# Two frequency rows in one PSUM tile, copied by two engines at once into halves of the partitions

## The chip, the cores and the metric

The kernel runs on one core of a Trainium2 chip (trn2). The metric is the device time of one execution in microseconds; the median of three runs is what versions are compared by. A profile records one further execution, with the start and length of each instruction on TensorE (PE, with its weight loads PEld), VectorE (DVE), ScalarE (ACT), GpSimd (POOL) and the queue of SyncE (SP), which issues the loads.

## The reference

The reference is four layers, each added to its input x of 2 images x 128 channels x 64 x 64 pixels, float32: an attention layer, a layer of convolutions, a convolution by Fourier transform and a second attention layer. Only the third, layer 2, is touched. It treats the 128 channels as 32 quaternions of four parts and multiplies in the frequency domain:

```python
xs = jnp.stack([x[:, :q], x[:, q:2 * q], x[:, 2 * q:3 * q], x[:, 3 * q:]])
Xs = jnp.fft.rfft2(xs, s=(GRID_H, GRID_W), axes=(-2, -1))
Ws = jnp.stack([kr_w + 1j * ki_w, kr_x + 1j * ki_x, kr_y + 1j * ki_y, kr_z + 1j * ki_z])
C = jnp.einsum('piohw,qbihw->pqbohw', Ws, Xs)
Pw = C[0, 0] - C[1, 1] - C[2, 2] - C[3, 3]
Px = C[0, 1] + C[1, 0] + C[2, 3] - C[3, 2]
...
o = jnp.fft.irfft2(P, s=(GRID_H, GRID_W), axes=(-2, -1))
```

For each of 64 x 33 frequencies this is a product of a 128 x 32 matrix of weights (real and imaginary) with the spectrum of both images, in four signed arrangements of the parts.

## The kernel before

Layer 2 is `_layer2`, L803. A first part normalizes X and transforms it along the height; the result is `y`, kept in SBUF. A last part transforms back along the height and adds to X. Between them stands the part that the change touches, L897 to L1117. It works on eight blocks `kb` of four frequency rows `m` and their four mirror images, so a block has two halves: first the products of the *direct* rows, then those of the *image* rows. In each half:

- `rows_of_weights` (L819) has SyncE load the weights of four rows, real and imaginary, 2112 KB each, into one of two buffers.
- `products` (L990) runs 17 steps, `j`, one for each pair of frequencies. A step is four matmuls with 32 columns each, one for each of four rows `s`; the trace has two instructions for each, so a step is eight. They multiply the weights by `e`, the copied and signed spectra, into one of four banks `z0` to `z12`, or, for the last step, into a bank of the pool `bank`. After every fourth step VectorE transposes a bank into `z` (L1017), and at the end it combines `z` to `pz` (L1025).
- Beside the products, `alongside` (L1075) takes steps of other generators, so that the next block is prepared and the last one is finished under the products: `rows_in` for two rows of the next block; `turned`, which transposes `pz` (L1037) and copies it to `pzt` (L1044, ScalarE); and in the direct half `back`, which transforms the last block back along the width (L1062) and copies it to `y` (L1065, ScalarE). `alongside` spreads a given number of steps over the 17, and takes what is left over after the last.

`rows_in` (L971) is the preparation. `transposed` (L909) turns a row of `y` by TensorE (L912) and ScalarE copies it to `yt` (L918). `transformed` (L921) multiplies it by a matrix, for both images, into a bank of the tag `pe` (L925), which has two buffers, so each of the two rows has its own. The bank then holds the spectrum of the direct row and of its image row. `copies` and `placed` (L979, L934) write it to `e` for both places. The four quaternion parts lie on four groups of 32 partitions, and each is needed in four arrangements `r` with signs `SIGN2`: part `p` of arrangement `r` comes from part `r ^ p`. That is 12 copies for a row and a place, of 136 elements: one of all 128 partitions with signs from a tile, one of 64 and ten of 32. `together` (L962) alternates two generators: ScalarE makes all copies of the first row (L948), VectorE all of the second (L950), four at a step. So `rows_in` has ten steps for two places, the last of each place without work.

The instructions of an engine run in the order in which the program was written (`_in_order`). Semaphores between the engines are set by the language's tile layer, which also gives out the buffers of a pool in turn: an instruction that needs a buffer waits for the last use of it.

For block 0 all four rows of the direct place are prepared before the first product, and those of the image place beside its direct half; its image half has two `rows_in` beside it, for block 1. Block 7 prepares nothing.

## Time and profile before

| | |
|---|---|
| median of 3 runs | 4103.53 us (4102.0 to 4110.83) |
| the profiled execution | 4101.59 us, of which the span of the profile is 4099.8 us |
| busy over the span | PE 3930.8 us (96%), DVE 3182.8 (78%), ACT 3230.9 (79%), POOL 72.5 (2%) |
| the stretch of the changed code | about 1918 to 2181 us of the span |
| copies to `e`, ScalarE | 384 instructions |
| copies to `e`, VectorE | 384 instructions |

Lines of the profile are read so. The page's second part cuts the span in 40 slices; a digit is the busy share in tenths. The view by stretch gives, for each stretch, its length, then busy microseconds and the count of instructions of PE, PEld, DVE, ACT and POOL, the clock that TensorE was granted, the share of the DMA engines and GB/s. A line of the waits names engine, tile and line that waited, then what ended the wait: microseconds in all, times, the longest. A line of the timeline is start, length, engine, line, instruction, output and input, count, and in brackets the idle time before it with what ended it. A line of the groups gives count, then busy microseconds and mean nanoseconds of one, then the idle time before them. A line of the DMA issues ends with the size in KB and the median time to landing in us.

### The profile page before, as it was taken

Reading aid. Unit: us, or ns where it says so; the run is one execution under the profiler, and the core shown is the slowest. Engines: PE = TensorE matmul, PEld = TensorE weight load, DVE = VectorE, ACT = ScalarE, POOL = GpSimd, SP = SyncE. Lnnn points to the kernel's source line nnn. Section 1 sums busy time; section 2 is a strip of 40 time slices with the busy share of each in tenths; the row PEclk is TensorE's granted clock in tenths of the full one; section 3 lists DMA queues with packets and bytes.
Section 4 is the critical chain, followed back from the end, with each engine's and each line's share of the span. In section 5 each row is a group of like instructions: output and inputs, shape, how many; then the busy total and the mean of one; then the engine's idle time right before and its main releaser. Section 6 shows DMA issues by size and latency. Waiting matters only on the chain. (4 is left out here: it accounts for less than half of the span.)

```text
span 4099.8 us, 83182 instructions
## 1 busy us (share of the span) xinstructions
PE 3930.8 (96%) x35790; PEld 1374.4 (34%) x35790; DVE 3182.8 (78%) x3526; ACT 3230.9 (79%) x3907; POOL 72.5 (2%) x145
## 2 busy tenths in 40 slices
PE   7999999989999998997898999999999999999998
PEld 4522222245222223445565232222222222222222
DVE  4689999856989998986775887777777777776666
ACT  4478888744888884334663899999999999999998
POOL 1001000000000001000000000000000000000000
PEclk9999999999999999998899999999999999999999
DMA  1199980000000000002673211120012101110000
GB/s 50 20 184 178 179 123 2 2 2 2 1 2 2 2 2 13 0 2 100 257 285 116 87 34 32 31 66 27 29 32 63 34 24 32 33 56 6 6 6 4
DMA packets 193133, 217.66 MB, mean 53 GB/s; under 512 B 30441, under 2 KB 154345, under 8 KB 188658
## 3 DMA queue, kind: packets, MB, share of 16 engines
q1 hardware_dynamic: 192754, 212.25, 20.2%
q8 instruction: 282, 4.62, 0.5%
q14 instruction: 97, 0.79, 0.1%
HBM read 178.64 MB, written 98.57 MB: 68 GB/s over the span
## 5 line engine op out<-in xcount | busy, mean ns | idle before, releaser
L2183 ACT ACTIVATE weights<-ps_s 128x1024 f32<-128x1024 f32 x1920 | 1781.7, 1066 | 77.0 <-PE ps_s L2169 76.9
L1381 ACT ACTIVATE weights<-ps_s 128x1024 f32<-128x1024 f32 x1024 | 993.4, 1024 | 170.4 <-PE ps_s L1372 152.3
L2192 PE MATMUL ps_acc<-weights,vt 128*32 128x512 f32 x8192 | 1093.8, 606 | 0.0
L1829 DVE TENSOR_TENSOR sums<-sums,weights 128x2048 f32<-128x2048 f32 x384 | 879.9, 2291 | 45.4 <-ACT weights L1381 9.1
L2169 PE MATMUL ps_s<-q,k 64*128 64x512 f32 x4096 | 831.4, 470 | 4.0 <-DMA k<-stack 2.8
L2169 PEld LDWEIGHTS ps_s<-q,k 64*128 64x128 f32 x4096 | 348.9, 184 | 937.2 <-ACT weights L2183 810.3
L1372 PE MATMUL ps_s<-q,k 32*64 32x512 f32 x8192 | 630.9, 614 | 4.6 <-ACT weights L1381 2.4
L1789 PE MATMUL ps_acc<-weights,vt 128*32 128x512 f32 x4096 | 551.7, 607 | 7.2 <-ACT used L1819 3.7
L2141 DVE SCALAR_TENSOR_TENSOR exp_z<-exp_z,exp_m 128x1024 f32<-128x1024 f32 x384 | 468.9, 1221 | 9.3
L2125 DVE TENSOR_SCALAR exp_i<-ps_s 128x1024 int32<-128x1024 f32 x128 | 156.7, 1224 | 217.2 <-PE ps_s L2169 217.0
L1372 PEld LDWEIGHTS ps_s<-q,k 32*64 32x64 f32 x8192 | 161.8, 130 | 435.6 <-PE ps_s L1372 337.1
L2192 PEld LDWEIGHTS ps_acc<-weights,vt 128*32 128x32 f32 x8192 | 161.9, 108 | 309.8 <-issue 309.4
L1789 PEld LDWEIGHTS ps_acc<-weights,vt 128*32 128x32 f32 x4096 | 81.2, 108 | 427.5 <-issue 404.0
L662 DVE SCALAR_TENSOR_TENSOR X<-g,w,X 128x2048 f32<-128x2048 f32 x84 | 197.3, 2350 | 2.6
L1829 DVE TENSOR_TENSOR sums<-weights 128x2048 f32<-128x2048 f32 x64 | 146.6, 2291 | 63.2 <-ACT weights L1381 62.9
L2145 DVE SCALAR_TENSOR_TENSOR weights<-exp_z,exp_i 128x1024 f32<-128x1024 f32 x128 | 156.8, 1225 | 15.6 <-ACT weights L2183 0.5
L1577 PE MATMUL ps_sp<-pad,diag 32*32 32x512 f32 x4608 | 158.9, 597 | 2.3 <-ACT q L1597 1.3
L2141 DVE SCALAR_TENSOR_TENSOR exp_z<-exp_m 128x1024 f32<-128x1024 f32 x128 | 155.8, 1218 | 0.0
L1008 PE MATMUL ps_z<-w_ri,e 128*32 128x128 f32 x2048 | 137.3, 408 | 14.5 <-DVE e L950 12.3
L1577 PEld LDWEIGHTS ps_sp<-pad,diag 32*32 32x32 f32 x4608 | 96.0, 103 | 53.1 <-issue 15.7
L950 DVE TENSOR_SCALAR e<-ps_pe 32x136 f32<-32x136 f32 (+1 forms) x352 | 104.4, 297 | 5.0
L948 ACT ACTIVATE e<-ps_pe 32x136 f32<-32x136 f32 (+1 forms) x352 | 99.3, 282 | 4.1
(296 smaller groups left out, 2801.4 us busy)
## 6 DMA issues: line engine op xcount, KB each, us to landing
w_ri<-w_r SPq DMA_DIRECT2D x16, 2112.0 KB, 8.1
w_ri<-w_i SPq DMA_DIRECT2D x16, 2112.0 KB, 13.4
stack<-qs SPq DMA_DIRECT2D x64, 256.0 KB, 2.1
q<-stack SPq DMA_DIRECT2D x128, 128.0 KB, 2.5
k<-stack SPq DMA_DIRECT2D x128, 128.0 KB, 2.5
stack<-ks SPq DMA_DIRECT2D x32, 256.0 KB, 2.2
w_r<-in_L_conv_kr_w SPq DMA_DIRECT2D x15, 528.0 KB, 13.7
w_r<-in_L_conv_kr_x SPq DMA_DIRECT2D x15, 528.0 KB, 13.3
```

What stands on the lines that cost most here:

```text
L662: nc.vector.scalar_tensor_tensor(xi, g[:, i : i + H // 2, j : j + W], w8[:, s : s + 1], xi, ALU.mult, ALU.add)
L1372: nc.tensor.matmul(ps[j // 2][to, j % 2, :], k[rows, kt * 128 + 64 * half : kt * 128 + 64 * half + 64], q[rows, qb * CH : (qb + 1) * CH], ...
L1381: nc.scalar.activation(w[:, 2 * p : 2 * p + 2, :], ps[p], AF.Exp)
L1577: nc.tensor.matmul(ps[r // 2][to, r % 2, :].rearrange("p (h w) -> p h w", w=W), diag[rows, grp, t, :], pad[rows, y0 : y0 + ROWS, t % 3 : t ...
L1789: nc.tensor.matmul(ac[n][rows, :], lhs(rows), w[:, j, :], start=first, stop=last)
L1829: nc.vector.tensor_add(parts[0].rearrange("p j c -> p (j c)"), t.rearrange("p j c -> p (j c)"), w.rearrange("p j c -> p (j c)"),)
L2125: nc.vector.tensor_scalar(i, ps.rearrange("p j c -> p (j c)"), EXP_SCALE, EXP_BIAS, ALU.mult, ALU.add)
L2141: nc.vector.scalar_tensor_tensor(z, x, n, m, ALU.add, ALU.mult)
L2145: nc.vector.scalar_tensor_tensor(w.rearrange("p j c -> p (j c)"), z, EXP_TERMS[-1], power, ALU.add, ALU.mult)
L2169: nc.tensor.matmul(ps[j // 2][:, j % 2, :], g.k[kt // 4][rows, j // 2, keys], g.q[qb][rows, j // 2, :], start=True, stop=True,)
L2183: nc.scalar.activation(w[0], ps[p], AF.Exp)
L2192: nc.tensor.matmul(g.ac[32 * j : 32 * j + 32, :], g.vt[:, kt, j // 2, i : i + 2, :].rearrange("p a d -> p (a d)"), w[:, i, :], start=(at = ...
```

## The change

Two rows now share one tile `pe` of two banks, with one buffer in place of two of one bank each. The matmul of an image writes its columns with steps, so that the two images' real and imaginary parts stand side by side, four to a frequency, as they stand in `e`. A copy then takes both rows at once, 272 elements. The work is divided by partitions and no longer by rows: ScalarE writes partitions 0 to 63, VectorE 64 to 127. For two rows and a place ScalarE makes 7 copies and VectorE 6. `e` of the image place keeps the rows in the order in which they come, and `products` reads them from the other end. `together` and `copies` are gone, and `rows_in` has eight steps.

```diff
-        def transformed(m, yt):
-
-            pe = bank("pe")
+        def transformed(m, yt, pe):
+
             for b in range(B):
                 nc.tensor.matmul(
-                    pe[:, b * 8 * PAIRS : (b + 1) * 8 * PAIRS],
+                    pe[:, :, b],
                     yt[:, b, :],
-                    k["fwd_w_both" if m else "fwd_w_ends"],
+                    k["fwd_w_both" if m else "fwd_w_ends"].rearrange("p (x c) -> p x c", c=2),
                     start=True,
                     stop=True,
                 )
-            return pe[:, : B * 8 * PAIRS].rearrange("p (b s f c) -> p b s f c", b=B, s=2, c=2)
-
-        def placed(kb, m, got, image, e, scalar):
-
+
+        def placed(m, got, image, e):
 
 
             row = (m - 1) % 4
-            s, row = (1, 3 - row) if image else (0, row)
 
             def copied(r, p, n=1):
                 to = slice(32 * p, 32 * p + 32 * n)
                 of = slice(32 * (r ^ p), 32 * (r ^ p) + 32 * n)
-                sign = signs if n == 4 else float(SIGN2[r][p])
-                out = e[to, row, :, 4 * r : 4 * r + 4].rearrange("p f (b c) -> p b f c", c=2)
-                sign = sign[to, :] if n == 4 else sign
-                if scalar:
-                    nc.scalar.mul(out, got[of, :, s], sign)
+                sign = signs[to, :] if r == 0 else float(SIGN2[r][p])
+                out = e[to, row : row + 2, :, 4 * r : 4 * r + 4]
+                if p < 2:
+                    nc.scalar.mul(out, got[of, :, image], sign)
                 else:
-                    nc.vector.tensor_scalar_mul(out, got[of, :, s], sign)
-
-            copied(0, 0, 4)
+                    nc.vector.tensor_scalar_mul(out, got[of, :, image], sign)
+
+            copied(0, 0, 2)
+            copied(0, 2, 2)
+            copied(2, 0)
             copied(2, 2, 2)
-            copied(2, 0)
             copied(2, 1)
             yield
             for r in (1, 3):
...
         def rows_in(kb, rows, places, es):
 
             yts = [transposed(m) for m in rows]
             yield
-            gots = [transformed(m, yt) for m, yt in zip(rows, yts)]
+            pe = psp.tile([128, 2, CH], F32, tag="pe", name="ps_pe", bufs=1)
+            pairs = pe[:, :, : B * 8 * PAIRS].rearrange("p m (sf b c) -> p m sf b c", b=B, c=2)
+            got = pe[:, :, : B * 8 * PAIRS].rearrange("p m (s f x) -> p m s f x", s=2, x=2 * B)
+            for n, (m, yt) in enumerate(zip(rows, yts)):
+                transformed(m, yt, pairs[:, n])
             yield
...
             for image in places:
                 if es[image] is None:
                     es[image] = ep.tile([128, 4, 2 * PAIRS, 8 * B], F32, tag="e", name="e")
-                yield from together(
-                    *(
-                        placed(kb, m, got, image, es[image], i % 2 == 0)
-                        for i, (m, got) in enumerate(zip(rows, gots))
-                    )
-                )
-
-        def products(ws, e, pz):
+                yield from placed(rows[0], got, image, es[image])
+
+        def products(ws, e, image, pz):
...
-                        e[:, s, 2 * j : 2 * j + 2, :].rearrange("p f x -> p (f x)"),
+                        e[:, 3 - s if image else s, 2 * j : 2 * j + 2, :].rearrange("p f x -> p (f x)"),
...
-            alongside(products(rows_of_weights(kb, False), e[0], pzs[0]), chain(*side), n)
+            alongside(products(rows_of_weights(kb, False), e[0], 0, pzs[0]), chain(*side), n)
...
-            alongside(products(rows_of_weights(kb, True), e[1], pzs[1]), chain(*side), n)
+            alongside(products(rows_of_weights(kb, True), e[1], 1, pzs[1]), chain(*side), n)
```

More of the change, by code (lines that the diff above doesn't have):

```diff
@@ L960, in placed @@
                 yield
-        def together(*gens):
-            gens = list(gens)
-            while gens:
-                for g in list(gens):
-                    if next(g, gens) is gens:
-                        gens.remove(g)
-                yield
         def rows_in(kb, rows, places, es):
@@ L974, in rows_in @@
             yield
-            gots = [transformed(m, yt) for m, yt in zip(rows, yts)]
+            pe = psp.tile([128, 2, CH], F32, tag="pe", name="ps_pe", bufs=1)
[3 more added lines that the diff above has]
+                transformed(m, yt, pairs[:, n])
             yield
-            yield from copies(kb, rows, gots, places, es)
-        def copies(kb, rows, gots, places, es):
             for image in places:
```

## The prediction

> **What bounds the kernel now.** I read the page's slices first, to see which engine holds each stretch, then the busy time by stretch around the changed code, then its instructions in order of time, then the clock after a wait, then the durations of the copies.

> ```profile
> span 4099.8 us, 83182 instructions
> PE   7999999989999998997898999999999999999998
> w_ri<-w_i SPq DMA_DIRECT2D x16, 2112.0 KB, 13.4
> ```

> TensorE is the busy engine nearly everywhere. The changed code runs from 1918 to 2181 us alone. The last line is half of a weight load: it lands 13.4 us after issue. The same stage by stretch (busy us and instructions of each engine, the granted clock, DMA share, GB/s):

> ```profile
> 1918.30:1970.00 51.70, 34.80 (x358) 22.80 (x358) 35.53 (x107) 32.90 (x110) 0.00 (x0) 0.79 0.30 115
> 1970.00:2153.60 183.60, 173.53 (x2061) 116.16 (x2064) 133.78 (x368) 114.69 (x347) 0.00 (x0) 0.92 0.70 276
> ```

> The first row is the fill (the first two row pairs and block 0), the second six like blocks, 1 to 6, at 183.6/6 = 30.6 us. There TensorE is busy 95%; VectorE (73%) and ScalarE (62%) work beside it. TensorE's waits in the second row:

> ```profile
> PE ps_z L1008 <- DVE e L950: 6.6, 6, 2.1
> PE ps_bank L1062 <- ACT y L1065: 4.8, 6, 0.8
> ```

> So at most 11.4 us can be won there, 0.3%. One block in order of time (TensorE, VectorE, ScalarE):

> ```profile
> 2050.17 0.64 PE L1008 MATMUL ps_z<-w_ri,e 128*32 128x128 f32 x8
> ...
> 2052.04 1.19 PE L925 MATMUL ps_pe<-consts,yt 128*128 128x136 f32 x8
> 2053.27 0.36 DVE L950 TENSOR_SCALAR e<-ps_pe,signs 128x136 f32<-128x136 f32 x1 [4.52 <-PE ps_pe L925]
> 2053.20 3.23 ACT L948 ACTIVATE e<-ps_pe 64x136 f32<-64x136 f32 x11
> 2060.10 0.58 ACT L1044 COPY pzt<-ps_bank 66x512 f32<-66x512 f32 x1
> ```

> The reader is to see that ScalarE and VectorE copy at the same time, each from its own bank, and that ScalarE's pzt copy comes only after its copies. Last, what follows a wait of TensorE (slices: busy us, granted clock, DMA share, GB/s):

> ```profile
> 1945.00:1947.00 2.00, 0.00 (x0) 0.54 0.88 338
> ...
> 1953.00:1955.00 2.00, 2.00 (x44) 1.00 0.97 405
> ```

> ```profile
> 1947.52 0.67 PE L1008 MATMUL ps_z<-w_ri,e 128*32 128x128 f32 x8 [4.38 <-DVE e L950]
> 1949.32 2.18 PE L925 MATMUL ps_pe<-consts,yt 128*128 128x136 f32 x8
> ...
> 1985.91 3.63 PE L1062 MATMUL ps_bank<-consts,pzt 66*128 66x128 f32 x16 [0.81 <-ACT y L1065]
> ```

> A wait of 4.38 us brings the clock to a half until some 5 us after its end. L925 then takes 2.18 us, not 1.19, and L1062 3.63, not 2.05; a product group (8 matmuls) starts every 0.5 us at either clock.

> **The change part by part.** Durations of what it replaces and of the nearest larger reads from PSUM (mean ns behind the comma):

> ```profile
> L950 DVE TENSOR_SCALAR e<-ps_pe 32x136 f32<-32x136 f32 x320 | 95.0, 297 | 4.5
> L948 ACT ACTIVATE e<-ps_pe 32x136 f32<-32x136 f32 x320 | 90.3, 282 | 3.7
> L948 ACT ACTIVATE e<-ps_pe,signs 128x136 f32<-128x136 f32 x32 | 12.1, 379 | 17.9 <-PE ps_pe L925 17.7
> L918 ACT COPY yt<-ps_bank 128x256 f32<-128x256 f32 x36 | 12.9, 374 | 26.8 <-PE ps_bank L912 26.3
> L1065 ACT COPY y<-ps_bank 128x512 f32<-128x512 f32 x14 | 10.1, 723 | 38.0 <-PE ps_bank L1062 38.0
> L876 DVE COPY gt<-ps_pt 128x512 f32<-128x512 f32 x1 | 0.7, 691 | 1.0 <-PE ps_pt L870 1.0
> ```

> *Count and length of copies.* For two rows and one place (direct or image) ScalarE and VectorE each issued 12 copies of 136 elements; now ScalarE issues 7 and VectorE 6 of 272. ScalarE: 374 ns at 256 elements and 587 at 512 (the copies L884 and L1140) give 0.83 ns an element, so 272 cost 0.395 us, with signs 0.49. VectorE: (691-297)/376 = 1.05 ns an element, so 0.44, with signs 0.50 (that copy took 0.36 behind a wait, 0.06 more). As busy time: 2.86 and 2.70 us a group against 3.6 and 3.7. Bounds: no cost for the added elements (0.28 and 0.30); strided as L1065 (0.47).

> *Side by side becomes one behind the other.* Both engines now read the same two-bank tile. In the built program each access to it from one engine waits for the last access from the other: A, D, A, D, AAA, DD, AA, DD (A a ScalarE copy, D a VectorE copy), and the next group's first A for the last D. That is 8 hand-overs a group. Hand-overs between these engines in this trace:

> ```profile
> 13.29 0.16 DVE L1508 SCALAR_TENSOR_TENSOR gn_shift<-gn_got 128x1 f32<-128x1 f32 x1 [0.67 <-POOL gn_got L1403]
> 13.49 0.81 ACT L1515 ACTIVATE g<-X,gn_shift,gn_got 128x512 f32<-128x512 f32 x1 [7.52 <-DVE gn_shift L1508]
> ```

> 13.45 to 13.49 is 0.04 us. Group: 2.86 + 2.70 + 8 x 0.04 + 5 x 0.01 between copies of one engine + 3 x 0.04 (a VectorE copy after a wait took 0.36, in a row 0.32) = c = 6.05 us, where the two together took 3.75. Bounds of c: 4.4 (elements free), 6.95 (strided, hand-overs 0.05 dearer, the length of a semaphore event on TensorE's queue). I take 6.05: its rows read PSUM on the same engines.

> [...] No row here shows two engines in one bank; the built waits are by bank.

> *Image half* (products of the mirrored rows; L1008 to L1008). Start to end of L925 is 3.05 us (2050.17 to 2053.23). Then 0.05, two groups 12.1, and 0.15 for a transpose of 0.72 that stands between the groups in VectorE's queue, of which the next A covers all but that: copies end at 15.35. The next direct half needs them for its rows 2 and 3. Behind ScalarE's last copy (14.35) queues the pzt copy, 0.58, which frees the bank for the last product (0.5 us): TensorE ends at 15.45. TensorE's own work is 11.3 (2050.17 to the end of the last product at 2060.95, and one L1037 of 0.56 that moves in from behind it).

> *Direct half.* VectorE still has two transposes of 0.72 and one of 0.28 after its last copy, which free the bank of the second row: TensorE waits about 0.75, L925 ends at 3.4. Two groups: 15.55; ScalarE's last copy 14.55; pzt 15.2. rows_in now has 8 steps, not 10, so the back-transforms (L1062, 2.05 each) stand in front of products 15 and 16 and not behind all 17; the 0.8 us wait for y between them goes, but they wait for pzt: 15.2 + 2.05 + 0.5 + 2.0 + 0.5 = 20.25. All other products are done beneath the copies. Behind a waiting VectorE copy stand its transposes of products (L1017); but for the one above, TensorE needs their banks only half a block later.

> *The clock.* TensorE now stands idle about 4 us twice a block: before the last product of the image half (own work done at 10.6, bank at 14.95) and before the back-transforms (10.9 to 15.2). By the 4.38 us wait each brings some 5 us of half clock. After the first, two transposes and most of L925 at the head of the direct half: +1.2. After the second, the first L1062 whole (+1.6) and half of the other (+0.8). Bounds: none, and everything on the path (L912 0.3, L925 1.0 in both halves, L1062 1.6 twice: +5.8). I take +3.7 with what is left at the head of the image half, by the wait of the nearest length.

> *Block*: 15.45 + 20.25 + 3.7 = 39.4, that is 4c + 15.2. Six blocks: 6 x 39.4 - 183.6 = +52.8 us.

> *Fill.* Two pairs come before the first product: the second pair's matmuls wait for the first pair's whole group (one pe buffer of two banks), so the first product's last rows come at 1920.6 + 6.05 + 1.7 + 6.05 = 1934.4, not 1929.7. Two more groups, with L912, yt and L925 ahead of the first (4.8) and L925 ahead of the second (1.2), end block 0's direct half at 1952.5, not 1947.5. Its image half takes two pairs, four groups, both L925 at half clock after long waits: 1952.5 + 4.4 + 12.2 + 2.3 + 12.1 = 1983.5, and 0.3 for the last product, against 1970.0: +13.8 us. Block 7 has no copies, but its first L1037 waits for VectorE's pz (1.59 us now), 1.0 longer.

> *At nothing:* products L1008 (same count); their row order 3-s (addresses only); SP's weight loads, issued when the last product of a half has read its buffer, 13.8 us with issue, under 15.45; without that cover TensorE would wait for them. L925's output with steps: between none and the half-clock row (2.18 against 1.19, +1 a pair, +15 in all); I take none, the column count is the same.

> *Sum:* 13.8 + 52.8 + 1.0 = +67.6. The profiled execution took 4101.6 us (span 4099.8), 1.9 below the median of 4103.5: 4169.2 on its own scale, 4171.1 on the median's. I say 4170.

> **Rivals.**
> 1. *Longer still (0.10).* Strided copies, hand-overs at 0.09: c = 6.95, 0.9 on 32 groups: 4199. For it: rows of 4 elements are written with gaps, as in L1065. Against it: so were the rows of 2 elements now, at 282.
> 2. *Slower, but by less (0.09).* The clock holds, as it did here after one in three of the 0.81 us waits: 4146; with c = 5.4 as well 4125. Against it: waits of 4 us.
> 3. *No difference (0.04).* Elements nearly free, c = 4.4: copies end at 12.2 in the image half and the weight load (13.8) sets it; direct half 16.95; TensorE hardly waits, so no clock is lost: 30.7 a block, 4103 to 4108. It decides at 4c + 11.5 = 30.6, c = 4.8. The rising rows (297 to 691, 374 to 587) speak against it.
> 4. *Faster (0.03).* The engines overlap after all: a group is then as long as its longer engine, below 3 us. TensorE's 11.4 us of waits go, but image halves of 11.3 meet the load of 13.8: direct halves become 12.1 of products and transposes and two L1062, 16.1; block 16.1 + 13.8 = 29.9, six blocks -4, the fill -5: 4094. The built waits speak against it.

> **How the numbers follow.** The forecast has 0.74. With c from 5.4 (a third of the added element cost gone) to 6.6 (ScalarE strided), 32 groups, its own range is 4149 to 4188. For 8 in 10 I reach down to rival 2 and up towards 1 and a strided L925: 4130 to 4196. 0.2% (8.2 us) is about what a measurement of this kernel tells from no change: slower by more 0.93, within 0.04, faster 0.03.

> **What would show it.** Right: copies of about 0.4 us with 272 elements, 13 a group, ScalarE waiting for VectorE's e and the reverse, some 250 times in all; blocks near 39 us; pzt starting right after ScalarE's last copy and TensorE waiting for it before the back-transforms; clock at a half there; the other stages unmoved. Wrong: ScalarE and VectorE copying at once, copies under 0.33 us, or TensorE waiting for a weight load.

## The result, and the profile after

The changed kernel takes 4178.81 us (median of 5 runs, 4175.64 to 4184.11) against 4103.53 us before (5 runs, 4100.01 to 4110.83): a ratio of 1.0183, 95% interval 1.0172 to 1.0193, so 75 us longer. The forecast was 4170, with a range of 4130 to 4196. The profiled execution after took 4184.11 us, the highest of the five; its span is 4182.2 us, 82.4 more than that of before. So the durations below are of an execution about 5 us longer than the median.

The page of after, its span and two of the rows of 40 slices (one digit for each 104.6 us):

```profile
span 4182.2 us, 82821 instructions
...
PE   7999999989999998996888899999999999999998
...
PEclk9999999999999999998778899999999999999999
```

Before, the row of the clock was this (the row of PE stands in the prediction):

```profile
PEclk9999999999999999998899999999999999999999
```

The two rows differ from those of before in slices 19 to 23 alone: TensorE is less busy there, at a lower clock. Measured from the first transpose of the part that the change touches (L912) to the first transpose of the last part of the layer, that stage took 270.8 us before (1918.31 to 2189.11) and takes 343.95 us now (1921.59 to 2265.54), 73.15 us more. The rest of the 82.4 us lies in other stages (this one begins 3.3 us later), and most of it is not in the medians, which are 75.3 us apart.

The same by stretch, as before: the fill, up to block 1, then blocks 1 to 6 (length, busy us and counts of PE, PEld, DVE, ACT, POOL, then clock, DMA share, GB/s):

```profile
1921.59:1987.22 65.63, 33.47 (x353) 22.84 (x357) 28.24 (x59) 27.68 (x70) 0.00 (x0) 0.78 0.17 67
1987.22:2230.57 243.35, 196.15 (x2068) 134.00 (x2064) 114.79 (x228) 98.46 (x228) 0.00 (x0) 0.77 0.54 215
```

Six blocks took 183.6 us and take 243.35. TensorE was busy 95% of them at a clock of 0.92; now it is busy 81% at 0.77. VectorE has become less busy, not more (47%, from 73%): no engine has taken over as the bound by its work. What did is in the waits of the stage (who waited for what: us in all, times, the longest):

```profile
DVE e L945 <- ACT e L943: 116.8, 117, 4.7
ACT e L943 <- DVE e L945: 82.3, 110, 1.9
...
PE ps_bank L991 <- ACT pzt L1027: 29.2, 7, 6.6
...
PE ps_bank L1045 <- ACT pzt L1027: 24.1, 7, 4.0
...
PE ps_pe L924 <- DVE e L945: 15.6, 3, 7.7
```

ScalarE and VectorE wait for each other 227 times. Before, the two engines never waited for each other's `e`, and of TensorE's three lines the last two stood at 0.2 and 0.9 us. The copies that do the waiting, by groups:

```profile
L943 ACT ACTIVATE e<-ps_pe 32x272 f32<-32x272 f32 x192 | 75.1, 391 | 70.1 <-DVE e L945 69.0
...
L945 DVE TENSOR_SCALAR e<-ps_pe 32x272 f32<-32x272 f32 x128 | 56.1, 439 | 53.8 <-ACT e L943 52.7
```

A copy of twice the elements costs ScalarE 391 ns (282 before) and VectorE 439 (297). So the copies fell from 7.3 us of engine time to 5.5 for two rows and a place, but one engine idles almost as long as it works. In order of time, the head of one group:

```profile
2054.67 0.48 ACT L943 ACTIVATE e<-ps_pe,signs 64x272 f32<-64x272 f32 x1 [1.97 <-PE ps_pe L924]
2055.19 0.51 DVE L945 TENSOR_SCALAR e<-ps_pe,signs 64x272 f32<-64x272 f32 x1 [2.89 <-ACT e L943]
2055.73 0.39 ACT L943 ACTIVATE e<-ps_pe 32x272 f32<-32x272 f32 x1 [0.57 <-DVE e L945]
2056.15 0.43 DVE L945 TENSOR_SCALAR e<-ps_pe 64x272 f32<-64x272 f32 x1 [0.46 <-ACT e L943]
```

Each copy starts 0.03 to 0.04 us after the end of the other engine's. The next group starts at 2060.52, 5.85 us after this one. What TensorE does meanwhile, from the end of an image half over the direct half of the next block:

```profile
2066.32 0.67 PE L991 MATMUL ps_bank<-w_ri,e 128*32 128x128 f32 x8 [3.74 <-ACT pzt L1027]
...
2069.39 2.09 PE L924 MATMUL ps_pe<-consts,yt 128*128 128x136 f32 x8
...
2082.93 3.78 PE L1045 MATMUL ps_bank<-consts,pzt 66*128 66x128 f32 x16 [3.99 <-ACT pzt L1027]
...
2087.24 3.78 PE L1045 MATMUL ps_bank<-consts,pzt 66*128 66x128 f32 x16
```

TensorE runs out of work twice a block and then waits 3.74 and 3.99 us for a pzt copy that stands in ScalarE's queue behind its last copy to `e`. What follows each wait is at half clock: L924 takes 2.09 us, not 1.19, and both back-transforms 3.78, not 2.05. The clock in slices of 2 us (length, TensorE's busy us, ..., granted clock, DMA share, GB/s):

```profile
2064.00:2066.00 2.00, 0.00 (x0) 0.00 (x0) 1.12 (x3) 1.10 (x3) 0.00 (x0) 0.60 0.02 8
2066.00:2068.00 2.00, 1.68 (x18) 0.88 (x18) 1.96 (x5) 0.75 (x2) 0.00 (x0) 0.50 0.08 21
2068.00:2070.00 2.00, 1.89 (x13) 1.11 (x13) 1.29 (x3) 0.75 (x2) 0.00 (x0) 0.50 1.02 237
2070.00:2072.00 2.00, 2.00 (x19) 1.71 (x22) 0.00 (x0) 0.48 (x1) 0.00 (x0) 0.69 1.02 439
...
2080.00:2082.00 2.00, 0.00 (x0) 0.00 (x0) 0.92 (x3) 1.01 (x4) 0.00 (x0) 0.87 0.02 8
2082.00:2084.00 2.00, 1.07 (x5) 1.07 (x6) 1.58 (x3) 1.34 (x3) 0.00 (x0) 0.50 0.00 0
2084.00:2086.00 2.00, 2.00 (x11) 2.00 (x11) 0.00 (x0) 0.00 (x0) 0.00 (x0) 0.50 0.00 0
...
2092.00:2094.00 2.00, 2.00 (x17) 1.27 (x14) 1.15 (x2) 0.74 (x2) 0.00 (x0) 0.50 0.83 203
2094.00:2096.00 2.00, 2.00 (x20) 1.73 (x23) 0.00 (x0) 0.41 (x1) 0.00 (x0) 0.72 0.94 397
```

After the first wait (its end is 2066.32) the half clock lasts until about 2071; after the second (2082.93) until about 2095, through 12 us in which TensorE is busy without a pause.

### The profile page after: what moved, and what is told of

Its sections match the earlier page's. It is cut to its first block, busy times and chain, and to the rows that moved or that the text cites. A ratio compares the mean times of both kernels' runs of the same rounds, so it can differ in the third digit from the quotient of the medians.

```text
span 4182.2 us, 82821 instructions
## 1 busy us (share of the span) xinstructions
PE 3960.8 (95%) x35790; PEld 1397.0 (33%) x35790; DVE 3155.7 (75%) x3334; ACT 3209.4 (77%) x3747; POOL 74.7 (2%) x145
## 5 line engine op out<-in xcount | busy, mean ns | idle before, releaser
L2128 DVE SCALAR_TENSOR_TENSOR weights<-exp_z,exp_i 128x1024 f32<-128x1024 f32 x128 | 156.8, 1225 | 15.2
L943 ACT ACTIVATE e<-ps_pe 32x272 f32<-32x272 f32 x192 | 75.1, 391 | 70.1 <-DVE e L945 69.0
L945 DVE TENSOR_SCALAR e<-ps_pe 32x272 f32<-32x272 f32 (+1 forms) x160 | 70.0, 438 | 68.4 <-ACT e L943 67.3
## 6 DMA issues: line engine op xcount, KB each, us to landing
w_ri<-w_r SPq DMA_DIRECT2D x16, 2112.0 KB, 8.2
w_ri<-w_i SPq DMA_DIRECT2D x16, 2112.0 KB, 13.7
w_r<-in_L_conv_kr_w SPq DMA_DIRECT2D x15, 528.0 KB, 12.8
```

What stands on the lines that cost most here:

```text
L2128: nc.vector.scalar_tensor_tensor(w.rearrange("p j c -> p (j c)"), z, EXP_TERMS[-1], power, ALU.add, ALU.mult)
```

## The experiments

The theory to be tested: the loss is the turn that two engines take at one tile. It has two parts, the copies in a row on the path, and the half clock that the resulting waits of TensorE bring. The rivals: another part of the change costs the time (the stepped output of L924, the count of steps, the longer copies), or the weight load does. All versions but "the back-transforms divided" are made from the changed kernel. In the table at the end of this section, as in the text where nothing else is said, a block is the mean of blocks 2 to 6, from the last product of one image half to that of the next.

### By rows again, but in one tile

ScalarE copies the first row and VectorE the second, as before the change; each row has a bank of its own, but both lie in one tile.

```diff
-                out = e[to, row : row + 2, :, 4 * r : 4 * r + 4]
-                if p < 2:
-                    nc.scalar.mul(out, got[of, :, image], sign)
-                else:
-                    nc.vector.tensor_scalar_mul(out, got[of, :, image], sign)
+                for i in range(2):
+                    out = e[to, row + i, :, 4 * r : 4 * r + 4]
+                    if i == 0:
+                        nc.scalar.mul(out, got[of, i, image], sign)
+                    else:
+                        nc.vector.tensor_scalar_mul(out, got[of, i, image], sign)
 
-            copied(0, 0, 2)
-            copied(0, 2, 2)
-            copied(2, 0)
+            copied(0, 0, 4)
             copied(2, 2, 2)
+            copied(2, 0)
             copied(2, 1)
```

> The changed kernel with the division undone: ScalarE copies the first row and VectorE the second, 136 elements, 12 copies each, each from its own bank, but still of one tile of two banks. The prediction gave the serial order to waits by bank; in the built program of this kernel the waits between the engines are all still there, so they go by tile. Theory (the alternation of the two engines, whatever they read, sets the time): copies take turns one by one, 12 x (0.29 + 0.34 + 2 x 0.04) = 8.5 us a group where the changed kernel had 5.86, over 32 groups +85 us: 4230 to 4280 us. Rival (the engines disturb each other in a bank, or the 272-element copies with their steps are what costs): with own banks and short copies the time falls to 4095 to 4130.

Measured: 4243.84 us (2 runs), 1.0332 of before (1.0311 to 1.0352). Its waits and a stretch of its two engines in order of time:

```profile
DVE e L946 <- ACT e L944: 144.3, 328, 4.6
ACT e L944 <- DVE e L946: 135.8, 338, 1.7
```

```profile
2042.39 0.28 ACT L944 ACTIVATE e<-ps_pe 64x136 f32<-64x136 f32 x1 [0.62 <-DVE e L946]
2042.69 0.29 DVE L946 TENSOR_SCALAR e<-ps_pe 64x136 f32<-64x136 f32 x1 [0.34 <-ACT e L944]
2043.02 0.28 ACT L944 ACTIVATE e<-ps_pe 32x136 f32<-32x136 f32 x1 [0.36 <-DVE e L946]
2043.33 0.29 DVE L946 TENSOR_SCALAR e<-ps_pe 32x136 f32<-32x136 f32 x1 [0.34 <-ACT e L944]
```

Two engines in two banks, and still each copy starts only after the other's last: the waits of the built program go by tile. The prediction said "by bank", which the changed kernel alone could not tell from "by tile", since both of its banks are read by both engines. Two engines did read two banks at the same time in the kernel before, where ScalarE's eleven copies from 2053.20 to 2056.43 ran beside VectorE's from 2053.27 on, and in the next version, where ScalarE's eleven from 2049.85 to 2053.00 ran beside VectorE's from 2049.93 on. ScalarE and VectorE in one bank at once no run here shows.

### By rows, a tile for each

The same, but each row has a tile of one bank. What stays of the change is the stepped output of L924, the eight steps and the order of rows in `e`.

```diff
-            pe = psp.tile([128, 2, CH], F32, tag="pe", name="ps_pe", bufs=1)
-            pairs = pe[:, :, : B * 8 * PAIRS].rearrange("p m (sf b c) -> p m sf b c", b=B, c=2)
-            got = pe[:, :, : B * 8 * PAIRS].rearrange("p m (s f x) -> p m s f x", s=2, x=2 * B)
-            for n, (m, yt) in enumerate(zip(rows, yts)):
-                transformed(m, yt, pairs[:, n])
+            pes = [bank("pe")[:, : B * 8 * PAIRS] for _ in rows]
+            got = [pe.rearrange("p (s f x) -> p s f x", s=2, x=2 * B) for pe in pes]
+            for m, yt, pe in zip(rows, yts, pes):
+                transformed(m, yt, pe.rearrange("p (sf b c) -> p sf b c", b=B, c=2))
```

> As the run above, but each row again in a tile of one bank; the matmuls write with steps, rows_in has 8 steps and e of the image keeps its order, as in the changed kernel. No wait between the engines is left in the built program. Theory: all of the loss is the taking of turns, so this stands with the kernel before, 4090 to 4108 us; image halves near 13.8 us, set by the weight load or by VectorE's copies. Rival A (the matmul's stepped output, the 8 steps with the back-transforms in front of products 15 and 16, or the rows' order costs): 4115 to 4150.

Measured: 4104.07 us (10 runs), 0.9993 of before (0.9982 to 1.0004): no difference. Between these two kernels only the tiles differ, and they are 140 us apart. So the loss is the turn taking, and the stepped output, the eight steps and the order of rows cost in sum nothing that can be measured. The waits of TensorE show one thing that was not there before:

```profile
PE ps_z L990 <- DMA w_ri<-w_i: 9.0, 3, 3.4
PE ps_z L990 <- DVE z L999: 8.4, 3, 3.0
```

With eight steps both back-transforms lie among the products of the direct half. Its image half is left with about 11.2 us of work (2015.29 to 2026.47, last product to last product), less than the 13.7 us that the weight load takes from issue to landing, and the direct half has 20.0. So TensorE waits for weights at the seam, as rivals 3 and 4 said it would. The profile puts three of the waits down to a transpose of VectorE, but that had ended 0.4 to 0.9 us before TensorE went on; behind the image halves of blocks 1 to 5 TensorE always went on 13.3 to 14.2 us after the issue of the load's second half (1985.23 to 1998.95 for the first).

### Two hand-overs instead of eight

The tile and the 13 copies as changed, but in another order: ScalarE's seven first, then VectorE's six.

```diff
             copied(0, 0, 2)
-            copied(0, 2, 2)
             copied(2, 0)
-            copied(2, 2, 2)
             copied(2, 1)
-            yield
             for r in (1, 3):
-                for p in range(4):
-                    copied(r, p)
-                yield
+                copied(r, 0)
+                copied(r, 1)
+            yield
+            copied(0, 2, 2)
+            copied(2, 2, 2)
+            copied(1, 2)
+            yield
+            copied(1, 3)
+            copied(3, 2)
+            copied(3, 3)
+            yield
```

> The changed kernel with the same 7 and 6 copies in another order: all of ScalarE's, then all of VectorE's, so 2 hand-overs a group and not 8. Theory (the sum of the copies sets the time, a hand-over costs 0.04 to 0.08): a group 5.4 to 5.6 us for 5.86; ScalarE's last copy, and with it the pzt copy, is done 1.8 us earlier in the half, so direct halves lose about 2.5 us and image halves 0.9; 4145 to 4165 us. Rival (the hand-overs themselves are dear, 0.2 us and more each): a group 4.6 us or less, 4120 us or less.

Measured: 4155.31 us (4 runs), 1.0122 of before (1.0101 to 1.0143), 24 us less than the changed kernel. ScalarE's side of two groups, and TensorE's waits:

```profile
2045.70 0.48 ACT L943 ACTIVATE e<-ps_pe,signs 64x272 f32<-64x272 f32 x1 [1.29 <-PE ps_pe L924]
2046.19 2.40 ACT L943 ACTIVATE e<-ps_pe 32x272 f32<-32x272 f32 x6
2051.43 0.48 ACT L943 ACTIVATE e<-ps_pe,signs 64x272 f32<-64x272 f32 x1 [2.83 <-DVE e L945]
```

```profile
PE ps_bank L996 <- ACT pzt L1032: 12.6, 7, 4.3
PE ps_bank L1050 <- ACT pzt L1032: 11.2, 7, 1.9
```

A group takes 5.73 us here, 0.13 less than with eight hand-overs: over 32 groups that is 4 us of the 24. The hand-overs themselves are cheap. The rest comes from where ScalarE's last copy stands: before VectorE's six, so the pzt copy behind it starts some 2 us sooner, and TensorE's two waits are 1.4 and 1.9 us, no longer 3.74 and 3.99 (the 4.3 is in block 0). The block went from 40.9 to 36.2 us. Over the six blocks (1983.50 to 2200.94) TensorE stood idle for 28.6 us, where it was 47.2, and was busy for 188.86 us with the same work, where it was 196.15, at a clock of 0.82 and not 0.77: so 18.6 of the 25.9 us are shorter waits and 7.3 are the clock.

### The waits filled

The changed kernel, but one product step in each half (the 15th in the direct half, the 16th in the image half) is issued nine times instead of once, with the same values, in blocks 0 to 6. It is 896 matmul instructions more, put where TensorE waits, so that it doesn't stand idle. The copies and their waits stay.

```diff
-                for s in range(4):
+                for s in list(range(4)) * (fill if j == 14 + image else 1):
...
-            alongside(products(rows_of_weights(kb, False), e[0], 0, pzs[0]), chain(*side), n)
+            alongside(products(rows_of_weights(kb, False), e[0], 0, pzs[0], 9 if nxt else 1), chain(*side), n)
...
-            alongside(products(rows_of_weights(kb, True), e[1], 1, pzs[1]), chain(*side), n)
+            alongside(products(rows_of_weights(kb, True), e[1], 1, pzs[1], 9 if nxt else 1), chain(*side), n)
```

> The changed kernel with TensorE kept busy where it stood idle: in blocks 0 to 6 the product step before each of the two long waits (step 14 of a direct half, step 15 of an image half) is issued nine times and writes the same values nine times, 8 x 0.48 = 3.9 us more work for waits of 3.7 to 4.0 us. Nothing else is moved; the output is the same. Theory (about 5.6 us a block are the half clock that follows the waits): the clock stays full from block 1 on, L1062's back-transforms take 2.05 and not 3.78 us, L925 1.19 and not 2.0, a block about 35 us and not 40.6: 4140 to 4155 us. Rival (the clock is low for another reason, or the excess over the copies is not the clock): the blocks stay at 40 us, 4175 us or more.

Measured: 4146.84 us (4 runs), 1.0099 of before (1.008 to 1.0118). More work, and 32 us less than the changed kernel by the medians (34 by the ratios). The stretch of six blocks of this kernel, and its direct half in order of time:

```profile
1980.60:2191.39 210.79, 207.13 (x2832) 134.72 (x2832) 114.90 (x228) 97.87 (x229) 0.00 (x0) 0.99 0.63 248
```

```profile
2061.16 4.82 PE L991 MATMUL ps_z<-w_ri,e 128*32 128x128 f32 x80
2066.25 2.05 PE L1045 MATMUL ps_bank<-consts,pzt 66*128 66x128 f32 x16 [0.26 <-ACT pzt L1027]
2068.23 0.64 PE L991 MATMUL ps_z<-w_ri,e 128*32 128x128 f32 x8
2068.80 2.05 PE L1045 MATMUL ps_bank<-consts,pzt 66*128 66x128 f32 x16
```

The clock is 0.99, the back-transforms take 2.05 us, and a block takes 210.79/6 = 35.13 us. In the changed kernel six blocks take 2230.57 - 1987.22 = 243.35, 40.56 each. So the half clock costs 5.4 us a block, and the copies in a row cost the other 35.13 - 30.6 = 4.5. This split takes the block of before as it was, with its clock of 0.92. By the version with the back-transforms divided, below, some 1.9 us of that block were half clock too; without them, an estimate, the copies in a row cost 6.4 us and the clock 3.5 more than before.

### A tile and an engine for each place

ScalarE copies the image place and VectorE the direct place, each from its own tile of one bank, both rows at once (272 elements). L924 becomes two matmuls of 68 columns for each image, and block 0 prepares both of its places ahead.

```diff
+            w = k["fwd_w_both" if m else "fwd_w_ends"].rearrange("p (s f c) -> p s f c", s=2, c=2)
+            for s in range(2):
+                for b in range(B):
+                    nc.tensor.matmul(pe[s][:, :, b], yt[:, b, :], w[:, s], start=True, stop=True)
...
+                for image in (1, 0):
+                    out = es[image][to, row : row + 2, :, 4 * r : 4 * r + 4]
+                    if image:
+                        nc.scalar.mul(out, got[image][of], sign)
+                    else:
+                        nc.vector.tensor_scalar_mul(out, got[image][of], sign)
...
+            pes = [bank("pe")[:, : B * 8 * PAIRS] for _ in range(2)]
+            got = [pe.rearrange("p (m f x) -> p m f x", m=2, x=2 * B) for pe in pes]
```

> Copies of both rows at once, 272 elements, as in the change, but the bank holds a place and not a row: ScalarE makes the 12 copies of the image place from one tile, VectorE the 12 of the direct place from another. It takes two matmuls of 68 columns for one of 136. For block 0 both places are prepared ahead, and nothing beside its direct half. No wait between the engines is left. Theory: long copies are no cost in themselves; a pair takes about 5.4 us on VectorE (0.50 + 11 x 0.44) for 7.5 before, blocks are set by TensorE and the weight load: 4090 to 4112 us (the added matmuls about 0.6 us a pair). Rival (272 elements with steps are dear beside another engine's copies): 4130 us or more.

Measured: 4092.49 us (5 runs), 0.9961 of before (0.9947 to 0.9975): faster by 0.4%. The copies by groups, then TensorE's waits in the like blocks:

```profile
L941 DVE TENSOR_SCALAR e<-ps_pe 32x272 f32<-32x272 f32 x160 | 70.0, 437 | 2.4
L939 ACT ACTIVATE e<-ps_pe 32x272 f32<-32x272 f32 x160 | 62.4, 390 | 1.9
```

```profile
PE ps_z L987 <- DVE pz L1004: 6.8, 3, 2.5
PE ps_z L987 <- DMA w_ri<-w_i: 5.0, 2, 2.8
```

The copies are as long as in the changed kernel, two rows at once as there, and the engines idle 2 us before them in place of 54 and 70. The idea of copying both rows at once is sound; sharing the tile was not. The block is 30.7 us, no less than before: TensorE still waits once a block at the end of the short image half (11.9 us). The profile names weights twice and VectorE three times, but in all five TensorE went on 13.7 to 14.4 us after the issue of the load's second half, and in those three VectorE had ended 0.4 to 0.8 us before: it is the weights each time. The gain lies in the fill and block 1: the last product of block 1 comes 69.4 us after the start of the stage (1986.57 - 1917.14), before the change 82.2 (2000.54 - 1918.31).

### The back-transforms divided over the halves

The kernel before, with the empty fourth step of each place left out of `rows_in`, and one back-transform in the direct half, the other in the image half.

```diff
-            gens = list(gens)
-            while gens:
-                for g in list(gens):
-                    if next(g, gens) is gens:
-                        gens.remove(g)
+            for _ in zip(*gens):
                 yield
...
+        def first_of(gen):
+            next(gen)
+            yield
...
+            rest = iter(())
             if before:
-                side += [turned(pzs[1], before[1]), back(kb - 1, *before)]
-                n += 6
+                rest = back(kb - 1, *before)
+                side += [turned(pzs[1], before[1]), first_of(rest)]
+                n += 5
...
-            side, n = [turned(pzs[0], direct)], 4
+            side, n = [rest, turned(pzs[0], direct)], 4 + (before is not None)
```

> The kernel before with two edits that leave its copies alone: rows_in without its two empty steps, and of the two back-transforms one stays in the direct half and one goes to the image half. Theory (with the 8 steps an image half of 11.3 us ends before its successor's weights are there, 13.8 us after their buffer came free; halves of equal length hide the load): direct 14.1, image 13.8, blocks of 28 to 28.5 us for 30.6: 4085 to 4095 us. Rival (VectorE's copies of the first row's neighbour, 7.5 us a half behind 3 us of preparation, end after the products): no gain, 4100 us or more.

Measured: 4087.97 us (7 runs), 0.9951 of before (0.9938 to 0.9965). Its six blocks:

```profile
1965.21:2133.21 168.00, 162.04 (x2065) 103.00 (x2069) 139.12 (x377) 113.28 (x349) 0.00 (x0) 1.00 0.79 311
```

The halves now take 13.3 to 14.8 us each, about the length of a weight load (13.6 us from issue to landing). Six blocks fall from 183.6 to 168.0 us and the clock is 1.00, where it was 0.92. TensorE is busy 162.04 us with 2065 instructions, where it was 173.53 with 2061: so 11.5 of the 15.6 us are the same work done faster, and 4 are shorter waits. The short waits of the kernel before, 0.8 to 2.1 us, had cost little by themselves and more by the clock behind them.

### Both

The tile and engine for each place, with the back-transforms divided (the same lines of `first_of` and `rest`, put into that kernel).

> The run with a bank and an engine for each place, and with the back-transforms divided over the halves as in the run beside it. There TensorE waited 2.5 to 2.8 us for the weights after image halves of 11.9 us. Theory: halves of about 14.6 and 13.9 us, no wait for weights, blocks of 28.5 us for 30.5: 4078 to 4086 us. Rival (the wait after the image half was not the load): as that run, 4090 us or more.

Measured: 4082.78 us (4 runs), 0.9944 of before (0.9925 to 0.9964). Its six blocks:

```profile
1961.02:2133.93 172.91, 170.07 (x2164) 113.82 (x2160) 115.40 (x229) 87.81 (x205) 0.00 (x0) 1.00 0.76 302
```

TensorE is busy 98% at a clock of 1.00. The block (28.8 us) is longer than in the last version. Most of that is L926 with twice the matmuls (33.9 us in the whole stage without the division, where L924 took 27.8 in the version with a tile for each row). The fill is shorter. It is the lowest of all medians here, and beats both kernels, but its interval and that of the version before it overlap almost wholly: the runs don't tell the two apart.

| version | us | ratio to before | block, us |
|---|---|---|---|
| before | 4103.53 | 1 | 30.4 |
| the change | 4178.81 | 1.0183 | 40.9 |
| by rows, one tile | 4243.84 | 1.0332 | 49.4 |
| by rows, a tile each | 4104.07 | 0.9993 | 30.5 |
| two hand-overs | 4155.31 | 1.0122 | 36.2 |
| the waits filled | 4146.84 | 1.0099 | 35.2 |
| a tile and an engine for each place | 4092.49 | 0.9961 | 30.7 |
| before, back-transforms divided | 4087.97 | 0.9951 | 27.8 |
| both | 4082.78 | 0.9944 | 28.8 |

## Why the prediction was right, and where it was not

The mechanism was right: two engines at one tile take turns, ScalarE's pzt copy comes late behind the turns, TensorE waits for it twice a block and loses its clock (0.77 over the six blocks, 0.92 before). The versions with a tile for each row and for each place show that the rest of the change, the stepped output and steps in the one, the copies of 272 elements in the other, is not what costs the time. Term by term, the stage in the two profiles:

| term | predicted, us | measured, us |
|---|---|---|
| fill, up to block 1 | +13.8 | +13.9 (65.63 against 51.69) |
| six blocks, copies in a row | 6 x (35.7 - 30.6) = +30.6 | 6 x (35.13 - 30.6) = +27.2 (with the waits filled) |
| six blocks, the clock | 6 x 3.7 = +22.2 | 6 x 5.43 = +32.6 (40.56 - 35.13) |
| block 7 and the last back-transforms | +1.0 | -0.5 (34.97 against 35.51) |
| sum | +67.6 | +73.2 |

- **The group, c.** Predicted 6.05 us, measured 5.86. ScalarE's copy was put at 0.395 and 0.49 us (0.391 and 0.484 measured), VectorE's at 0.44 and 0.50 (0.439 and 0.507), a hand-over at 0.04 (0.03 to 0.04). Most of the surplus was the 3 x 0.04 added for VectorE copies behind a wait: here they took no longer than in a row (0.43 us behind a wait, 0.90 and 0.88 for two in a row). The rest lies in the hand-overs and in the copies. With 5.86 the block without clock loss is 4 x 5.86 + 11.5 = 34.9, where 35.13 was measured with the waits filled.
- **The clock: the term that was mis-sized.** "The first L1062 whole (+1.6) and half of the other (+0.8)" rested on "each brings some 5 us of half clock". That held for the first wait (from 2066.32 until about 2071) and not for the second, where the clock came back 12 us after the wait: both back-transforms took 3.78 us, and the head of the next image half ran slow too. It cost 5.43 us a block, near the 5.8 named as the upper bound, and makes 10 us too little in the sum.
- **"The built waits are by bank".** They are by tile, as two rows in two banks of one tile showed (666 waits between the two engines). Here both lead to the same order, so no number changed; for another layout of the same tile it would have.
- **Block 7.** Its first transpose of pz (L1037, now L1020) waits 2.00 us for VectorE, 0.4 more than before and not 1.0, and the end of the stage is otherwise a little shorter.
- **At nothing.** Stepped output of L924, order of rows, eight steps: in sum nothing, by the version with a tile for each row (0.9993). Hidden weight loads: no wait for them in the changed kernel; where the turn taking was gone they did appear, 2.6 to 3.4 us behind the image halves of blocks 1 to 5.
- **"At most 11.4 us can be won there".** This counted TensorE's waits in the six blocks and not the half clock behind them. With the back-transforms divided, the same six blocks became 15.6 us shorter, 11.5 of it in TensorE's busy time.
- **The rivals.** *Longer still* fell: copies took 391 ns and hand-overs 0.04 us. *Slower, but by less*, 4146 with the clock holding, did not happen; when the waits were filled so that it held, at 0.99, the time was 4146.84. So its price was near and its condition wrong; that the two agree to 1 us is luck, since the price was made with a group 0.19 us too long, some 6 us over 32 groups. *No difference* fell with copies of 391 and 439 ns. *Faster*, engines overlapping at 4094, did not happen in this tile; with a tile for each engine they did overlap, at 4092.49. That is near by luck too: the block was put at 29.9 us and was 30.7, and the fill at -5, where the stage up to the end of block 1 became 12.8 us shorter.

Offsetting misses are part of the closeness: the copies were 3.4 us too dear, block 7 1.5, and the clock 10.4 too cheap. The median stood 8.8 us above the forecast.

## What to carry to other kernels

When a change lets two engines read one tile, look at the waits of the built program before counting instructions: here they serialize by tile, and halving the copies could not make up for the two engines taking turns. Ask next what stands in the slower queue behind the work that now comes late, since it is that (here one copy of 0.58 us) for which the bounding engine waits. And price a wait of TensorE with the half clock behind it: in six blocks of the changed kernel that was 32.6 us, and in those of the kernel before, waits of 0.8 to 2.1 us brought 11.5.

## What the runs showed of the hardware that was not expected

```profile
2048.18 2.05 PE L1062 MATMUL ps_bank<-consts,pzt 66*128 66x128 f32 x16 [0.81 <-ACT y L1065]
```

- After a wait of 3.99 us the granted clock stayed at 0.50 for some 12 us of uninterrupted TensorE work, most of it the back-transforms (inputs on 66 partitions); after one of 3.74 us, followed by products and transposes, it was back about 5 us after the wait's end. In both the clock fell about 2 us after TensorE had stopped (by the shares of the slices, 1.8 and 2.5). So it fell before TensorE had been idle for a whole beat (3.41 us), and a whole beat of unbroken work did not always bring it back: between 2084.9 and 2091.7 lie two in which TensorE was busy without a pause, and the clock stayed at 0.50. What decides at which beat it changes no run here shows. Whether the kind of matmul decides it was not tried: with the waits filled, the same back-transforms ran at a clock of 1.00 (2066 to 2070), so they don't take it away by themselves.
- To repeat products in place of waiting, 896 instructions more, made the kernel 32 us faster.
- A hand-over between ScalarE and VectorE through a semaphore cost 0.03 to 0.04 us; six fewer in a group saved 0.13 us.
